# Spreading loads and stores of a Haar and convolution kernel over its pieces, and padding the rows of two inputs

## The chip, the cores and the metric

The kernel runs on one core of a Trainium2 chip. The metric is the device time of one execution in microseconds; lower is better. Engines are named as in the profile: PE is the matrix engine, PEld its weight loads, DVE the vector engine, ACT the scalar engine, POOL the general engine, and SP the engine that issues every DMA of this kernel.

## The reference

An image batch `x` of shape (4, 64, 256, 256) passes through four layers. Layers 0, 2 and 3 are global convolutions of each channel with a separable filter, computed by a small network of sines and a decay; the reference does it with transforms of twice the length, and adds `x` times a bias. Layer 1 works in the Haar domain:

```python
f1 = haar2d(x)
acc = jnp.zeros_like(f1[:, :conv_w.shape[1]])
for i in range(v.shape[0]):
    f3 = f1 * v[i]
    f4 = jnp.einsum('bchw,oc->bohw', f3, conv_w[i])
    f5 = jnp.sign(f4) * jax.nn.relu(jnp.abs(f4) - tau[i])
    acc = acc + f5
y = haar2d(acc, inverse=True)
return y + x
```

`v` and `tau` have one value for each of the 256 x 256 coefficients; `conv_w` mixes the 64 channels, for each of two terms `i`.

## The kernel before, in words

Everything is 32-bit floating point. The convolutions are products with triangular Toeplitz matrices, first along rows and then along columns; a tile of a filter's Toeplitz matrix (`toep`) is loaded from a table of repeated filters in DRAM. The batch is cut into two groups of two images each (`GROUPS`, `NB`), a group into 32 rounds of two channels (`ROUNDS`, `CI`). One round's tile has 128 partitions of 8 x 256 values, 8 KB to a partition, 1 MB in all.

There are three phases, written as lists of pieces of Python code that issue instructions:

- Phase a, 64 rounds: load `x`, convolve (matmuls `a1ps` and `a2ps`, ACT copies, DVE adds the bias term), Haar along rows on POOL (L341, L343), Haar along columns on PE (`a3ps`, L305), scale on DVE (L474), store to `coef` in DRAM.
- Phase b, once for each group, 64 steps of 128 units: load coefficients of all channels (`ft`, L545) and a step's `v` and `tau` (L557, one tile `v`), mix the channels on PE (L603, result in one PSUM tile `f4`), multiply by `v` on DVE (L622), sign and magnitude on ACT (L628, L637), subtract `tau` and threshold on DVE (L642, L647), add on POOL (L662, L665, L666), store to `mixed` (L671). For the second group half of the units skip the threshold: they are copied (L619) and stored to `unshrunk` (L679), and are thresholded late, in phase c.
- Phase c, 64 rounds of 18 pieces j = 0 to 17: load `g` from `mixed` in four DMAs of 256 KB (L746), scale it on ACT (L359), inverse Haar along rows on POOL (L382, result `ci`), along columns on PE (`c0ps`), then the last two convolutions (`c1r`, `c1c`, `c2r`, `c2c`), and store `out` (L867).

The function `beside` interleaves two lists: after each piece of the main list it issues as many pieces of the side list as keep both in proportion. Phase b of the first group runs beside phase a of the second group; phase b of the second group runs beside phase c of the first group; phase c of the second group runs alone. Every engine executes its instructions in the order in which the pieces issue them, so the place of a call in a piece is the place in the engine's queue. SP has one queue as well: a DMA that waits for a buffer or for its data holds up all DMAs issued after it. `AHEAD` is 3, and `alone` is 32, the first round of the second group.

Pools give a tile one of `bufs` buffers in turn; `ft` has four, `v` three, `g` three, `out` two. `load_f(s + 3)` loads the coefficients for three steps later and has to wait until POOL has added the previous step's, which read the same buffer. In phase c, piece (t, j) handles several rounds at once: it loads `g` for round t + 3 and scales it, runs POOL's steps for round t + 2, and the second convolution and the store for round t − 2.

Of the kernel before, what the change touches and what calls it, by code (L numbers as in the profile page):

```python
# [41 lines left out]
F32 = mybir.dt.float32  # L42
# [5 lines left out]
P = 128  # L48
B, C, N = 4, 64, 256

ROW = 64
BLOCKS = N // ROW
# [13 lines left out]
GROUPS = 2  # L66
NB = B // GROUPS
CI = 4 // NB
M = CI * NB

ROUNDS = C // CI
HALVES = 2 * ROUNDS
STEPS = C
# [4 lines left out]
AHEAD = 3  # L78
SHRINK = (1, 2, 3, 5, 6, 10, 11, 12, 14, 15)
W = 2 * N  # L80
# [4 lines left out]
IMAGES = (GROUPS, NB, ROUNDS, CI, BLOCKS, ROW, N)  # L85
TO_ROUNDS = (0, 2, 1, 5, 3, 4, 6)
# [4 lines left out]
C2 = float(np.float32(round((2.0 * math.pi - C1) * 2**21) / 2**21))  # L91
# [5 lines left out]
def conv_haar_kernel(  # L97
    ctx: ExitStack, tc: tile.TileContext, x, zT, w1, wbd, cols, wo, decay, wo_first, decay_first, bias, forward, inverse, wrow, pack, v, v_rows, out
):
    nc = tc.nc  # L100
# [7 lines left out]
    def coefficients(name):  # L108
        return dram.tile([CI, STEPS // 2, PAIR], F32, tag=name, name=name)

    coef = [coefficients(f"coef{g}") for g in range(GROUPS)]
    mixed = [coefficients(f"mixed{g}") for g in range(GROUPS)]
# [9 lines left out]
    def big(tag, name, bufs):  # L122
        return ac.tile([P, 2 * M, N], F32, tag=tag, name=name, bufs=bufs)

# [13 lines left out]
    def load_x(t):  # L138
        grp, r = divmod(t, ROUNDS)
        xs = big("in", f"x_{t}", 3)  # L140

        n = CI if grp == 0 else 2 * M
        for k in range(0, 2 * M, n):
            nc.sync.dma_start(xs[:, k : k + n], x[grp, r, :, k : k + n])
        return xs

    def load_toeplitz(l, t):
# [172 lines left out]
    def forward_free(src, dst, name):  # L320
# [4 lines left out]
        while half > 0:  # L325
            sums = nxt = None
            if half > 1:
                nxt = ac.tile([P, 2 * M, half], F32, tag=f"h{half}", name=f"{name}{half}", bufs=1)
                sums = nxt
# [25 lines left out]
    def scales(src):  # L355

        half = 2
        while half < N:
            nc.scalar.mul(diffs(src, half), diffs(src, half), math.sqrt(half))  # L359
            yield  # L360
            half *= 2

    def inverse_free(src, dst, name, engine):
# [5 lines left out]
        while half < N:  # L369
            o = dst  # L370
            if half < HALF:
                o = ac.tile([P, 2 * M, 2 * half], F32, tag=f"h{2 * half}", name=f"{name}{2 * half}", bufs=1)
            d = diffs(src, half)
# [27 lines left out]
    def run(ops, count):  # L401
        for _ in range(count):
            next(ops, None)

    def all_rows(grp_tile, r, images, joined):

        parts = images.rearrange("(m q) (h n) k -> q m h (n k)", q=2, h=2)
        n = NB * W
        pairs = []
        for q in range(2):  # L410
            for h in (slice(0, 2),) if joined else (slice(0, 1), slice(1, 2)):
                at = grp_tile.offset + ((h.start * 2 + q) * ROUNDS + r) * n
                rows = [[PAIR, P // 2], [2 * ROUNDS * n, h.stop - h.start], [1, n]]
                pairs.append((bass.AP(grp_tile.tensor, at, rows), parts[q][:, h]))
        return pairs
# [105 lines left out]
    def phase_b(grp):  # L521
# [4 lines left out]
        def raw(u):  # L526
            return grp == GROUPS - 1 and u % 2 == 1 and FULL <= u // 2 < STEPS
        st = [dict() for _ in range(STEPS)]
# [10 lines left out]
        def load_f(s):  # L539
            if s >= STEPS:  # L540
                return
            d = st[s]
            d["f"] = bp.tile([P, NB, W], F32, tag="ft", name=f"ft_{grp}_{s}", bufs=4)
            rows, f = step_of(coef[grp], s, d["f"])
            nc.sync.dma_start(f, rows)  # L545

        def load_v(s):
            if s >= STEPS:
                return
            d = st[s]  # L550
            d["v"], d["tau"] = [], []

            def fetch(first, count, tag):
                n = 2 * count * W
                t = bp.tile([P, count, 2, W], F32, tag=tag, name=f"{tag}_{grp}_{first}_{s}", bufs=3)
                at = v.offset + s * P * 4 * W + first * 2 * W
                nc.sync.dma_start(t.rearrange("p i k w -> p (i k w)"), bass.AP(v.tensor, at, [[4 * W, P], [1, n]]))  # L557
                d["v"] += [t[:, i, 0] for i in range(count)]
                d["tau"] += [t[:, i, 1] for i in range(count)]

            fetch(0, 2 if grp < GROUPS - 1 else 1, "v")
            if grp == GROUPS - 1 and not raw(2 * s + 1):
                fetch(1, 1, "raw")
# [117 lines left out]
        def piece(u, j):  # L681

            s, i = divmod(u, 2)
            if j == 0:
                if u < units:
                    multiply(u)
                if 0 < u <= units:
                    less(u - 1)
                if 1 < u <= units + 1:
                    add(u - 2)  # L690
                if i == 0 and s == 3:
                    part()
                    store(0)
                    store(1)
                if i == 0 and s > 3 and not raw(2 * s - 3):
                    store(s - 2)
                if i and raw(2 * s - 1):
                    store(s - 1)
            elif j == 1:
                if u + 1 < units:  # L700
                    mix(u + 1)
                if u < units:
                    sign(u)
                if i and s < STEPS and grp == GROUPS - 1:
                    store_raw(s)
                if 0 < u <= units:
                    threshold(u - 1)
                if i == 0 and s > 0:

                    load_v(s + 2)  # L710
                    load_f(s + 3)
            else:
                if u < units:
                    magnitude(u)
                if i == 0 and s < STEPS:
                    exchange(s)
# [16 lines left out]
    def phase_c():  # L733


        total = GROUPS * ROUNDS
        alone = total - ROUNDS
        st = [dict() for _ in range(total)]

        def load(t):  # L740
            if t >= total:
                return
            st[t]["g"] = big("in", f"g_{t}", 3)
            st[t]["scales"] = scales(st[t]["g"])
            for rows, g in all_rows(mixed[t // ROUNDS], t % ROUNDS, st[t]["g"], False):
                nc.sync.dma_start(g, rows)  # L746

        def load_raw(t):
            if alone <= t < total:
                r = st[t]["raw"] = late["sb"].tile([P, 2 * M, N], F32, tag="raw", name=f"raw_{t}", bufs=2)  # L750
                for rows, to in all_rows(unshrunk, t % ROUNDS, r, False):
# [40 lines left out]
        def scaled(t, count):  # L792
            if count and 1 < t < total:
                run(st[t]["scales"], count)
# [68 lines left out]
        def store(t):  # L863
            if t < total - 1:
                n = 2 * CI if t < alone else CI
                for k in range(0, 2 * M, n):
                    nc.sync.dma_start(out[t // ROUNDS, t % ROUNDS][:, k : k + n], st[t]["y"][:, k : k + n])  # L867
            st[t].clear()

        R1, C2, R2, C1 = 0, BLOCKS + 1, 2 * BLOCKS + 1, 3 * BLOCKS + 2  # L870

        def piece(t, j):
            flush()
            if j == 0:
                if t == 0:
                    load(2)
                sums(t + 2)
            if j == (BLOCKS if t == 0 else 1):
                load(t + 3)
            if j == 2:  # L880
                filters(t + 1, 1)
            if j == C2 + BLOCKS + 1 and t > 1:
                store(t - 2)
            if j == R2 + BLOCKS:
                filters(t, 2)
            first = t == alone - AHEAD
            if t >= alone - AHEAD:
                if j == 0 and first:
                    load_raw(alone)
                    load_rows()  # L890
                if j == 2 and first:
                    scale_rows()
                if j == BLOCKS + 1:
                    load_raw(t + AHEAD + 1)
                shrink(t + AHEAD, j - 2 * first)
            if R1 <= j < R1 + BLOCKS:
                if t < total:
                    rows(t, 1, j - R1)
            elif C2 <= j < C2 + BLOCKS:
                if 1 < t:  # L900
                    columns(t - 2, 2, j - C2)
            elif R2 <= j < R2 + BLOCKS:
                if 0 < t <= total:
                    rows(t - 1, 2, j - R2)
            elif j >= C1:
                if t < total:
                    columns(t, 1, j - C1)
            else:
                product(t + 1, int(j > BLOCKS))
            if t == 0:  # L910
                scaled(3, 2 * (2 * BLOCKS <= j < C1))
                scaled(2, int(j > 0))
            else:
                scaled(t + 3, {8: 3, 9: 2, 15: 1, 16: 1}.get(j, 0))
            if j > 0:
                step(t + 2, 1)

# [40 lines left out]
    a, head = a[-2 * A_PIECES :], A_PIECES + BLOCKS  # L958
# [134 lines left out]
```

## Time and profile before

| what | value |
|---|---|
| median of 3 runs | 2593.26 us (2591.77 to 2598.52) |
| profiled execution | 2595.18 us, its span 2591.5 us |
| mean granted PE clock | 0.977 |
| PE busy | 2324.7 us, 90% |
| PE weight loads | 1892.3 us, 73% |
| DVE busy | 1858.3 us, 72% |
| ACT busy | 1329.6 us, 51% |
| POOL busy | 2067.0 us, 80% |
| DMA | 685.23 MB, mean 264 GB/s |

The busy share is a mean over stages with different limits. The profile also cuts the span into 40 slices of 64.8 us and gives each engine's busy share in tenths for each; these rows and the busy times of single stretches are what to read first. A wait list says which engine waited for which, with the time in total, the number of times and the longest. "issue" stands for time in which an engine waited for nothing that the profile shows.

### The profile page before, as it was taken

To read this page: it belongs to the slowest core of one execution; us is meant where nothing else is said; L and a number is where in the kernel's file an instruction comes from. 1 tells how busy PE (TensorE), PEld (TensorE's weight loads), DVE (VectorE), ACT (ScalarE), POOL (GpSimd) and SP (SyncE) were. 2 spreads that over 40 slices of the span, in tenths; PEclk is the share of its full clock that TensorE was granted. 3 is DMA by queue.
4 is the path that set the end of the run, shared out by engine and by line. 5 is a ranking of instruction groups with operands and counts; after the bars stand their busy time and mean duration, and the time that the engine had idled before them with its cause. 6 is when DMAs were issued, how large, how long until landed. Compare 5 with 4: busy or idle time off the path is not lost.

```text
span 2591.5 us, 118522 instructions
## 1 busy us (share of the span) xinstructions
PE 2324.7 (90%) x53292; PEld 1892.3 (73%) x53292; DVE 1858.3 (72%) x2049; ACT 1329.6 (51%) x2187; POOL 2067.0 (80%) x2428
## 2 busy tenths in 40 slices
PE   5999998778888888757999999999989999999999
PEld 4887787444454445546777787787889999999998
DVE  2555445799999999646677677667757787777863
ACT  1221112566666666225666666666656556555552
POOL 1898887899999999757676877767779999999991
PEclk8999999999999999978999999999999999999999
DMA  7676898699999999555998989889876666666653
GB/s 209 219 245 232 287 304 293 248 346 317 348 324 329 346 321 331 184 191 184 328 320 304 330 302 313 309 313 315 289 221 219 212 203 222 210 205 210 215 166 112
DMA packets 203676, 685.23 MB, mean 264 GB/s; under 512 B 29289, under 2 KB 30826, under 8 KB 190755
## 3 DMA queue, kind: packets, MB, share of 16 engines
q1 hardware_dynamic: 203171, 677.67, 76.6%
q8 instruction: 418, 6.85, 1.1%
q14 instruction: 87, 0.71, 0.1%
HBM read 427.93 MB, written 249.63 MB: 261 GB/s over the span
## 4 chain that ended last, share of the span: by engine, by line
PE 53%; DVE 17%; POOL 9%; DMA 9%; issue 6%; ACT 3%; SPq 1%; DVEq 0%; ACTq 0%; POOLq 0%
PE c2c L293 9%; PE c2r L293 9%; PE c1r L293 8%; PE c1c L293 7%; PE a1ps L293 6%; PE a2ps L293 5%; PE f L603 4%; PE c0ps L305 3%; DVE m L647 3%; DVE x L622 3%; DMA v<-in_v 3%; POOL fw L341 2%; DVE a L642 2%; POOL f L343 2%; PE a3ps L305 2%
## 5 line engine op out<-in xcount | busy, mean ns | idle before, releaser
L382 POOL TENSOR_TENSOR i<-i,g 128x16 f32<-128x16 f32 x744 | 411.9, 574 | 27.7 <-ACT g L359 0.6
L293 PEld LDWEIGHTS a2ps<-toep,ay 64*64 64x64 f32 x8192 | 309.6, 137 | 158.0 <-DVE f L474 85.5
L293 PE MATMUL a2ps<-toep,ay 64*64 64x128 f32 (+3 forms) x8192 | 357.5, 306 | 46.6 <-DVE f L474 41.8
L603 PE MATMUL f<-ft,mix 64*64 64x512 f32 x2048 | 297.6, 619 | 109.5 <-DVE x L622 96.7
L293 PEld LDWEIGHTS a1ps<-toep,x 64*64 64x64 f32 x8192 | 293.6, 134 | 88.1 <-issue 43.7
L293 PE MATMUL a1ps<-toep,x 64*64 64x128 f32 (+3 forms) x8192 | 339.0, 300 | 18.6 <-DMA x<-in_x 13.8
L293 PEld LDWEIGHTS c2c<-toep,ch 64*64 64x64 f32 x8192 | 309.7, 134 | 54.1 <-issue 19.1
L293 PEld LDWEIGHTS c1c<-toep,ch 64*64 64x64 f32 x8192 | 306.6, 134 | 52.8 <-issue 17.5
L382 POOL TENSOR_TENSOR ci<-i,g 128x1024 f32<-128x1024 f32 x124 | 336.3, 2732 | 4.6
L293 PE MATMUL c1r<-toep,z 64*64 64x256 f32 (+3 forms) x8192 | 320.4, 300 | 19.2 <-ACT z L827 10.8
L293 PEld LDWEIGHTS c1r<-toep,z 64*64 64x64 f32 x8192 | 299.4, 135 | 47.6 <-issue 22.4
L293 PE MATMUL c2c<-toep,ch 64*64 64x128 f32 (+3 forms) x8192 | 320.7, 299 | 9.6 <-ACT ch L839 6.5
L293 PE MATMUL c1c<-toep,ch 64*64 64x192 f32 (+3 forms) x8192 | 316.9, 298 | 9.3 <-ACT ch L839 7.0
L441 ACT COPY ay<-a1ps 128x512 f32<-128x512 f32 x256 | 137.4, 589 | 351.8 <-PE a1ps L293 351.2
L293 PE MATMUL c2r<-toep,cy 64*64 64x128 f32 (+3 forms) x8192 | 311.9, 297 | 6.5 <-issue 5.9
L293 PEld LDWEIGHTS c2r<-toep,cy 64*64 64x64 f32 x8192 | 294.2, 134 | 30.5 <-issue 18.8
L665 POOL TENSOR_TENSOR gt<-m,ft 128x512 f32<-128x512 f32 x128 | 163.3, 1276 | 185.5 <-DVE m L647 179.1
L628 ACT ACTIVATE m<-x 128x1024 f32<-128x1024 f32 x194 | 206.1, 1063 | 193.6 <-DVE x L622 86.2
L839 ACT COPY ch<-c2r 128x512 f32<-128x512 f32 x256 | 137.5, 590 | 239.2 <-PE c2r L293 238.9
L474 DVE TENSOR_TENSOR f<-a3ps,wrow_sb 128x512 f32<-128x512 f32 x256 | 161.3, 682 | 132.6 <-PE a3ps L305 132.6
L622 DVE TENSOR_TENSOR x<-f,v 128x1024 f32<-128x1024 f32 x192 | 233.4, 1216 | 21.2 <-PE f L603 20.4
L839 ACT COPY ch<-c1r 128x512 f32<-128x512 f32 x256 | 137.8, 593 | 205.4 <-PE c1r L293 205.0
(83 smaller groups left out, 4001.2 us busy)
## 6 DMA issues: line engine op xcount, KB each, us to landing
toep<-filt SPq DMA_DIRECT2D x384, 224.0 KB, 5.4
ft<-coef SPq DMA_DIRECT2D x128, 512.0 KB, 7.7
v<-in_v SPq DMA_DIRECT2D x64, 1024.0 KB, 9.1
mixed<-gt SPq DMA_DIRECT2D x128, 512.0 KB, 7.4
g<-mixed SPq DMA_DIRECT2D x256, 256.0 KB, 5.3
x<-in_x SPq DMA_DIRECT2D x128, 256.0 KB, 4.9
coef<-f SPq DMA_DIRECT2D x128, 256.0 KB, 4.3
x<-in_x SPq DMA_DIRECT2D x32, 1024.0 KB, 8.6
```

What stands on the lines that cost most here:

```text
L293: nc.tensor.matmul(ps[r][half(c), j % 2, k * ROW :], data[half(r), c, k, bass.ts(j, ROW)], t(r, c)[:, : N - k * ROW], start=k == 0, stop=k ...
L305: nc.tensor.matmul(ps[r][half(c)].rearrange("p h k -> p (h k)"), matrix[half(r)], pairs(r, c).rearrange("p h k -> p (h k)"), start=True, s ...
L341: nc.gpsimd.tensor_tensor(diffs, even, odd, ALU.subtract)
L382: engine.tensor_tensor(to, s, d, op)
L441: later(lambda y=y, ps=ps: nc.scalar.copy(y, ps))
L474: later(lambda f=f, ps=ps, w=w: nc.vector.tensor_tensor(f, ps, w, ALU.mult))
L603: nc.tensor.matmul(un[u]["f4"][half(q), b, :], mixers[0][half(r), bass.ts(i, C)], st[s]["f"][half(r), b], start=True, stop=True, tile_posi ...
L622: nc.vector.tensor_tensor(un[u]["x"], un[u]["f4"], both(u, "v"), ALU.mult)
L628: nc.scalar.activation(un[u]["m"], un[u]["x"], AF.Sign)
L647: nc.vector.scalar_tensor_tensor(un[u]["m"], un[u]["a"], 0.0, un[u]["m"], ALU.max, ALU.mult)
L665: nc.gpsimd.tensor_tensor(g[:, 0], m[:, 0], st[s]["f"][:, 0], ALU.add)
L839: later(lambda y=y, ps=ps: nc.scalar.copy(y, ps))
```

## The change

There are three parts.

First, the arrays `x` and `v` in DRAM get rows of 8 KB and 512 bytes of zeros, so that row starts are 8704 bytes apart and no longer 8192. The same bytes are loaded in DMAs of the same sizes. `out` keeps its shape.

Second, in phase c of the first group, the four loads of `g` for a round are issued in pieces 1, 3, 5 and 7 in place of all in piece 1 (except in round 0 and in the rounds from `alone - AHEAD` on); the two halves of a store of `out` are issued in pieces 10 and 12 in place of both in piece 10; and the first five scalings of `g` on ACT go from pieces 8 and 9 to pieces 11 and 12 in all rounds but round 0.

Third, in phase b of the second group, `load_f(s + 3)` moves from the second third of a step's first unit, directly behind `load_v(s + 2)`, to the last third of its second unit, four pieces later. In the first group it stays.

```diff
+PAD = 128
...
-            nc.sync.dma_start(xs[:, k : k + n], x[grp, r, :, k : k + n])
+            at = x[grp, r, :, k * N : (k + n) * N]
+            nc.sync.dma_start(xs[:, k : k + n].rearrange("p n k -> p (n k)"), at)
...
-                at = v.offset + s * P * 4 * W + first * 2 * W
-                nc.sync.dma_start(t.rearrange("p i k w -> p (i k w)"), bass.AP(v.tensor, at, [[4 * W, P], [1, n]]))
+                at = v.offset + s * P * (4 * W + PAD) + first * 2 * W
+                rows = bass.AP(v.tensor, at, [[4 * W + PAD, P], [1, n]])
+                nc.sync.dma_start(t.rearrange("p i k w -> p (i k w)"), rows)
...
                 if i == 0 and s > 0:
 
                     load_v(s + 2)
+                    if grp < GROUPS - 1:
+                        load_f(s + 3)
+            else:
+                if i and s > 0 and grp == GROUPS - 1:
                     load_f(s + 3)
-            else:
                 if u < units:
                     magnitude(u)
...
-        def load(t):
+        def load(t, k=slice(0, 4)):
             if t >= total:
                 return
-            st[t]["g"] = big("in", f"g_{t}", 3)
-            st[t]["scales"] = scales(st[t]["g"])
-            for rows, g in all_rows(mixed[t // ROUNDS], t % ROUNDS, st[t]["g"], False):
+            if k.start == 0:
+                st[t]["g"] = big("in", f"g_{t}", 3)
+                st[t]["scales"] = scales(st[t]["g"])
+            for rows, g in all_rows(mixed[t // ROUNDS], t % ROUNDS, st[t]["g"], False)[k]:
                 nc.sync.dma_start(g, rows)
...
-                    nc.sync.dma_start(out[t // ROUNDS, t % ROUNDS][:, k : k + n], st[t]["y"][:, k : k + n])
+                    stores.append(lambda k=k, y=st[t]["y"]: nc.sync.dma_start(out[t // ROUNDS, t % ROUNDS][:, k : k + n], y[:, k : k + n]))
             st[t].clear()
+            for put in stores[: len(stores) if t >= alone else 1]:
+                put()
+            del stores[: len(stores) if t >= alone else 1]
...
-            if j == (BLOCKS if t == 0 else 1):
-                load(t + 3)
+            if t == 0 or t >= alone - AHEAD:
+                if j == (BLOCKS if t == 0 else 1):
+                    load(t + 3)
+            elif j in (1, 3, 5, 7):
+                load(t + 3, slice(j // 2, j // 2 + 1))
+            if stores and j == C2 + BLOCKS + 3:
+                stores.pop(0)()
...
-                scaled(t + 3, {8: 3, 9: 2, 15: 1, 16: 1}.get(j, 0))
+                scaled(t + 3, {11: 3, 12: 2, 15: 1, 16: 1}.get(j, 0))
...
+    def padded(rows):
+
+        return f(np.concatenate([rows, np.zeros((*rows.shape[:-1], PAD), np.float32)], axis=-1))
...
-        "x": f(a["x"].reshape(IMAGES).transpose(TO_ROUNDS).reshape(GROUPS, ROUNDS, P, CI * BLOCKS, N)),
+        "x": padded(a["x"].reshape(IMAGES).transpose(TO_ROUNDS).reshape(GROUPS, ROUNDS, P, 2 * M * N)),
...
-        "v": f(np.repeat(v[:, :, None], C, axis=2)),
+        "v": padded(np.repeat(v[:, :, None], C, axis=2).reshape(STEPS * P, 4 * W)),
```

More of the change, by code (lines that the diff above doesn't have):

```diff
@@ L737, in phase_c @@
         alone = total - ROUNDS
+        stores = []
         st = [dict() for _ in range(total)]
-        def load(t):
+        def load(t, k=slice(0, 4)):
             if t >= total:
                 return
-            st[t]["g"] = big("in", f"g_{t}", 3)
-            st[t]["scales"] = scales(st[t]["g"])
-            for rows, g in all_rows(mixed[t // ROUNDS], t % ROUNDS, st[t]["g"], False):
+            if k.start == 0:
+                st[t]["g"] = big("in", f"g_{t}", 3)
+                st[t]["scales"] = scales(st[t]["g"])
+            for rows, g in all_rows(mixed[t // ROUNDS], t % ROUNDS, st[t]["g"], False)[k]:
                 nc.sync.dma_start(g, rows)
@@ L1086 @@
     ]
-    args.append(nc.dram_tensor("out", arrays["x"].shape, F32, kind="ExternalOutput").ap())
+    args.append(nc.dram_tensor("out", (GROUPS, ROUNDS, P, CI * BLOCKS, N), F32, kind="ExternalOutput").ap())
     with tile.TileContext(nc) as tc:
```

## The prediction

> **What bounds the kernel now.** I read the page's slices first, then the busy time by stretch, then the waits inside the stretches that are not full.
>
> ```profile
> PE   5999998778888888757999999999989999999999
> DVE  2555445799999999646677677667757787777863
> DMA  7676898699999999555998989889876666666653
> ```
>
> A slice is 64.8 us. There are four stages: the first group's forward rounds (slices 1 to 6), the second group's beside the first group's mixing (7 to 16), the first group's inverse beside the second group's mixing (18 to 29), and the second group's inverse alone (to the end). The change is aimed at the third.
>
> ```profile
> core 0: us, PE busy (x) PEld busy (x) DVE busy (x) ACT busy (x) POOL busy (x), PEclk, DMA share, GB/s
> 270.00:390.00 120.00, 112.62 (x2868) 96.41 (x2864) 58.05 (x88) 21.57 (x40) 100.86 (x175) 1.00 0.94 303
> 520.00:1000.00 480.00, 391.61 (x6380) 233.31 (x6372) 459.08 (x470) 311.40 (x386) 434.58 (x474) 0.99 0.95 334
> 1225.00:1850.00 625.00, 586.18 (x13752) 487.63 (x13756) 444.21 (x422) 396.38 (x691) 457.33 (x513) 0.99 0.91 317
> 1950.00:2560.00 610.00, 608.29 (x16508) 577.24 (x16504) 460.61 (x487) 339.64 (x631) 538.58 (x540) 1.00 0.63 200
> ```
>
> The last stage has PE busy 608.3 of 610 us: nothing there can be won. In the second, DVE is busy 459.1 of 480 us (96%); its largest wait in that stretch is 16.6 us for ACT's magnitude, in 30 waits of at most 0.9 us, and none of its listed waits is for a DMA. So DMA, though 95% busy, does not set that stage. The third stage belongs to PE, which idles 625.0 − 586.2 = 38.8 us:
>
> ```profile
> PE f L603 <- DVE x L622: 15.4, 14, 2.3
> PE c1r L293 <- issue: 7.6, 9, 1.6
> PE c2r L293 <- issue: 5.9, 6, 1.7
> PE c2c L293 <- issue: 3.0, 4, 1.4
> PE c1c L293 <- issue: 2.2, 4, 0.9
> PE f L603 <- issue: 2.0, 1, 2.0
> ```
>
> (columns: us, times, longest). "issue" sums to 20.7 us in 24 stalls; 15.4 us are DVE being late with `x`. The second kind is no matter of transfers: before several of these, L642 (mean 1582 ns here, 1233 ns in the second stage) had taken over 2 us while POOL ran its 128x1024 step of L382 (mean 2816 ns).
>
> What is "issue"? PE's instructions come through DMA queue 8 (page: 418 packets, 6.85 MB, so 16 KB each). In the packet records PE's longer issue stalls mostly begin and end around such a packet and end 1.3 to 1.45 us after it lands. One case: packets of queue 8 start at 1506.5, 1510.8 and then only 1518.3, a gap of 7.5 us where 625/108 = 5.8 us is the mean; PE stalls 1.28 us from 1519.25. What SP had issued just before:
>
> ```profile
> 1506.47 3.28 SPq L746 DMA_DIRECT2D g<-mixed  x4
> 1509.85 1.20 SPq L155 DMA_DIRECT2D toep<-filt  x2
> 1511.15 1.01 SPq L557 DMA_DIRECT2D v<-in_v  x1
> 1512.27 0.54 SPq L545 DMA_DIRECT2D ft<-coef  x1
> 1513.27 0.57 SPq L671 DMA_DIRECT2D mixed<-gt  x1
> 1514.32 1.05 SPq L679 DMA_DIRECT2D unshrunk<-raw  x1
> ```
>
> That is 1024 + 448 + 4 x 512 = 3520 KB in 8.9 us, 405 GB/s asked of engines that move 317 in this stage. Other stalls (1532.4, 1456.3, 1634.1) also follow a burst of `g`; I take the backlog of a burst to hold up the fetch.
>
> **What the Trainium skill says.** *Runtime: NRT & Kernel Launch*, "Instruction fetch mechanics": the sequencer streams instructions in 16 KiB blocks through its own DMA queue, mostly hidden. The trace agrees on size and queue, not on hidden. *DMA: Bandwidth & Descriptors*, "Queues, rings and completion order": an engine alternates between its queues by packet, so a backlog should delay a fetch little; the 7.5 us gap above speaks against that, without proving what delayed it. The same page, "Latency and other measured facts": row pitches at large powers of two slowed copies, a few KiB of padding cured it and +192 B did not; its pitches start at 512 KiB. Here the pitch is 8 KB and the pad 512 B, so it is only a hint. The packet records add to it: in 520 to 1000 us an 8 KB packet (`v`, `x`) takes 309 ns at the median but 391 in the mean, 581 at the ninetieth percentile, while 4 KB packets (159, 170, 169) in the same stretch hardly vary. Yet rows of `ft` and `mixed` lie 4 KB apart, a power of two as well, so that the pitch is the cause is open. *SBUF — State Buffer*, "Who interferes with whom": a DVE instruction with two SBUF inputs blocks against a GpSimd one that reads SBUF; the 1582 ns of L642 agree.
>
> **The change part by part.** The sum is against the profiled execution, 2595.2 us (span 2591.5); the median of the three runs, 2593.3, lies 1.9 below it.
>
> *Padded `x` and `v`.* The same packets, 512 B apart. If the 8 KB mean falls from 391 to some 320 ns, the second stage's DMA share falls by 9125 x 71 ns / 16 / 480 us = 8 points, and buys nothing, because DVE's order of work repeats there every 9.4 us: 0 us (+3 to −5). In the first stage 2 KB packets take 106 ns where the median is 84: 0.26 of the share becomes 0.21, and 0.94 falls to some 0.89. PE idles 7.4 us in 270 to 390, 5.8 of it issue, 1.6 for `x`; I take −3 (0 to −7). At the start PE waits 9.3 us for `x`, behind the broadcast of the filters: −1 (0 to −3). In the third stage `v` is 58 x 128 packets of 4 KB; a saving of 40 ns each is 7424 x 40 ns / 16 = 19 us of 625, 3 points of 91, counted with the next part.
>
> *Loads of `g` in pieces j = 1, 3, 5, 7; half of `out` two pieces later; `ft` four pieces later.* Every issue remains (0.5 to 0.6 us of SP each, SP is not full); what goes is three of four `g` loads out of a burst, one of two stores, and `ft` from behind `v`. A round takes some 25.5 us here (24 rounds from the `g` load at 1222.7 to that at 1835.1), a piece 1.4 us, so 1024 KB are asked for over 8.5 us in place of 3. SP now waits 56.3 us at `ft` (L545) for POOL's L665, and toep, `g` and `out` queue behind it. After the move it meets the same event two pieces later at the store of `mixed` (L671, now 19.0 us on POOL), when it has mostly happened: that wait shrinks, and the store of `out` (L867, 99.5 us for DVE `o`), which only follows its producer, stays. `ft` is used two steps on, some 18 us after its new place, and lands in 7.2. I take half of the 20.7 us of issue stalls away: −10 (0 to −20). What is late next is DVE: its 15.4 us stay, and could grow a little where PE comes sooner.
>
> *Scales at j = 11, 12 instead of 8, 9.* The same ACT instructions. The last `g` load has four pieces, 5.7 us, to land before the first scale; before, the last of the burst had 6.6 to 13 us as read from the trace, and ACT waited for it only once after 1300 us (1.7 us). It lands in 6.2 now, alone a little sooner, and SP is usually ahead by some us. Behind ACT's wait stand the sign, magnitude and copies, then DVE's L642. +1 (0 to +12). POOL takes up the tile only in the next round, after all scales.
>
> *Transitions and last stage.* Loads of the last rounds keep their burst; the 7.1 us that ACT waits at 1885 stay: 0 (±2).
>
> Sum: −1 − 3 + 0 − 10 + 1 = −13, so 2582.2 for the profiled execution and **2580 us** as a median.
>
> **The rivals.** *Nothing moves* (24%): the fetch is late for a reason of its own, or DMA stays at 0.9 because no byte is taken away. For it: the second stage has 0.95 without harm to DVE; queues alternate by packet. Against: the last stage, at 0.63, has no issue stall listed although PE uses up instructions faster there. It gives −2 to 0 beside the first stage: about 2592. *ACT waits for the fourth `g`* (14%): it decides when landing exceeds 5.7 us plus SP's lead. With a landing of 9.4 (the longest in this stage before) and no lead, 3.7 us in each of some 25 rounds are 92 us of ACT, which idles 37%; if DVE and PE take over a fifth of it, +18, less 5 won: 2606, slower. The 1.7 us once speak against. *All of it goes* (10%): issue stalls vanish in both stages and some of `x`: −3 − 7 − 20 − 3 = −33, 2560. The forecast itself has 52%, 2571 to 2588. That the padding does nothing is a part of the first rival.
>
> **How the numbers follow.** I take 0.3%, 7.8 us, as what a measurement of this kernel can tell from no change; faster is below 2585.5. Of the forecast's 52% some 44 lie below; with the 10 and a little of the first rival, 56%. Slower: 14 and 2 of the rest, 16%. Same: 28%. The range leaves out the upper part of the slow rival and the tail below all stalls gone: 2560 to 2601.
>
> **What would show it.** Right: 8 KB packets near 320 ns in the mean; DMA share below 0.89 and "issue" near 10 us in 1225 to 1850; L545's wait for POOL gone; the second stage's step still 9.4 us. Wrong: "issue" at 20 us with `g` spread (first rival); ACT `g` <- DMA `g` above 25 us (second); the second stage shorter by over 5 us, which would mean that DMA did set it.

## The result and the profile after

The changed kernel takes 2586.21 us (median of 13 runs) beside 2594.36 us for the kernel before (13 runs on the same chip): a ratio of 0.9964 with a 95% interval of 0.995 to 0.9977. That is 0.36% or some 9 us (the medians lie 8.2 us apart); the forecast was 13. The profiled execution has a span of 2583.6 us against 2591.5 before, 7.9 less. The total came out nearly right, and by luck: the time was won in another place than the one forecast.

The slices of the kernel after, in the rows shown of before:

```profile
PE   5999999678888888757999999999989999999999
DVE  2555445799999999646677777766757777777763
DMA  7676998699999999555988999988876666666653
```

In slices 18 to 29, at which the spreading was aimed, PE's row is as it was. DMA's row there is no lower. The same stretches as before, by busy time:

```profile
core 0: us, PE busy (x) PEld busy (x) DVE busy (x) ACT busy (x) POOL busy (x), PEclk, DMA share, GB/s
270.00:390.00 120.00, 113.52 (x2870) 95.27 (x2866) 57.10 (x87) 21.81 (x41) 100.36 (x175) 1.00 0.95 311
520.00:1000.00 480.00, 390.73 (x6382) 231.96 (x6372) 459.07 (x470) 311.36 (x386) 434.60 (x474) 0.99 0.95 334
1225.00:1850.00 625.00, 586.26 (x13670) 480.16 (x13666) 442.48 (x420) 393.28 (x686) 449.56 (x510) 0.99 0.91 315
1950.00:2560.00 610.00, 610.00 (x16828) 557.63 (x16823) 430.93 (x494) 340.97 (x640) 544.04 (x542) 1.00 0.63 203
```

First, the third stage (third row): PE is busy 586.26 us where it was 586.18, DMA's share is 0.91 as before, and the matmuls in the stretch are 13670 where they were 13752. Nothing was won there. Second, the last row: PE's busy time rises by 1.7 us only, but the count in brackets goes from 16508 to 16828 matmuls in the same 610 us, 1.9% more work, and DVE's busy time falls by 30 us. The last stage became faster, and a busy share of 99.7% had hidden that there was something to win.

Cutting the trace at matmuls that stand for the same work in both kernels (the first mixing matmul, the first `c0ps`, the `c0ps` with which round 32 begins, the last matmul) gives each stage's length:

| stage | before, us | after, us | difference |
|---|---|---|---|
| first group's forward rounds | 436.8 | 435.4 | −1.4 |
| second group's forward rounds beside mixing | 681.0 | 682.5 | +1.5 |
| first group's inverse beside mixing | 817.4 | 820.3 | +2.9 |
| second group's inverse alone | 651.7 | 640.8 | −10.9 |

The differences sum to −7.9, the difference of the spans. Against my sum: −4 was forecast for the first stage, −9 for the third, 0 for the last.

PE's waits in 1225 to 1850 us after the change:

```profile
PE f L607 <- DVE x L626: 12.2, 12, 2.7
PE c1r L296 <- issue: 11.7, 14, 2.4
PE c1c L296 <- issue: 3.5, 5, 1.1
PE f L607 <- issue: 2.7, 3, 1.6
...
PE c2c L296 <- issue: 1.5, 3, 0.9
PE c2r L296 <- issue: 1.1, 2, 0.8
```

"issue" sums to 20.5 us in 27 stalls; before it was 20.7 us in 24. Spreading the bursts took none of it away. ACT's waits in the same stretch answer the rival that ended slower:

```profile
...
ACT g L362 <- DMA g<-mixed: 0.3, 1, 0.3
```

ACT waits 0.3 us for a load of `g`, once (10.4 us in three waits before). So ACT loses nothing by the later landing.

**Where the last stage won.** Half a round takes 9.59 us there, as the distance between `c0ps` pairs. Before, 14 of the 64 took 10.2 or 10.5 us; those are seven rounds with about 1.55 us lost in each, 10.9 us. After, none did. One of them, at 2105 us, in the timeline of before:

```profile
start us, us, engine line op out<-in xcount [idle before <-releaser]
...
2104.28 1.61 ACT L359 ACTIVATE g<-g 128x512 f32<-128x512 f32 x2
...
2105.96 4.69 POOL L806 TENSOR_TENSOR g<-g,shrunk 128x1024 f32<-128x1024 f32 x2 [0.43 <-ACT g L359]
...
2108.33 3.42 DVE L781 TENSOR_TENSOR x<-raw,rows 128x1024 f32<-128x1024 f32 x1
...
2111.84 1.03 ACT L783 ACTIVATE shrunk<-x 128x1024 f32<-128x1024 f32 x1 [1.55 <-DVE x L781]
...
2113.70 0.59 ACT L839 COPY ch<-c1r 128x512 f32<-128x512 f32 x1
```

The columns are start, duration, engine, line and operation, with the wait ahead of it in brackets. POOL's row is two instructions of 128x1024 in 4.69 us; in the instruction records the second begins at 2108.29 and lasts 2.36 us. DVE's L781, which also reads two SBUF operands, starts at 2108.33, 0.04 us behind it, and takes 3.42 us in place of 1.22, its shortest in this stage: the 2.32 us that POOL's instruction still has to run, and 1.10 us more. ACT stands 1.55 us idle for its result, and ACT's copy `ch`, queued behind, is late for PE's weight loads. The same round in the timeline of after:

```profile
start us, us, engine line op out<-in xcount [idle before <-releaser]
...
2104.66 1.62 ACT L362 ACTIVATE g<-g 128x512 f32<-128x512 f32 x2
...
2106.36 5.68 POOL L815 TENSOR_TENSOR g<-g,shrunk 128x1024 f32<-128x1024 f32 x2 [0.47 <-ACT g L362]
...
2108.20 1.62 DVE L790 TENSOR_TENSOR x<-raw,rows 128x1024 f32<-128x1024 f32 x1
...
2110.05 1.04 ACT L792 ACTIVATE shrunk<-x 128x1024 f32<-128x1024 f32 x1
...
2111.90 1.10 ACT L848 COPY ch<-c1r 128x512 f32<-128x512 f32 x2
```

PE's `c1r` begins at 2106.57 before and at 2106.50 after, so the two timelines can be laid over each other. ACT's last scaling of `g`, which releases POOL, ends 0.39 us later, and POOL starts 0.40 us later: the five moved scalings, 0.55 and 0.61 us of ACT's time, now stand among the copies just ahead of it (at 2101.37 and 2102.74), while before they ran in a gap at 2094.28. DVE arrives while POOL's first instruction is still running, goes next, and takes 1.62 us; now POOL's pair is the one that is stretched, to 5.68 us, and no half round is longer for it. ACT's copy `ch` comes 1.8 us earlier. The Trainium skill says in *SBUF — State Buffer*, "Who interferes with whom", that a DVE instruction with two SBUF inputs contends with a GpSimd (POOL) one that reads SBUF, and that the order of issue decides which of the two is blocked. The two timelines agree.

So do the records of all fourteen traces of this case, 64 of these DVE instructions in each. 580 of the 896 took over 1.3 us; every one of them started while a POOL instruction ran, and took the rest of that instruction plus 1.08 to 1.10 us. Only at the very start of a POOL instruction can DVE still go first: of the 45 that started less than 0.025 us behind it, 44 took under 1.3 us; of the 45 from 0.025 to 0.045 us, 20 did; of the 166 from there to 0.3 us, none. The kernel before stands on this edge: up to 0.032 us behind, its L781 took 1.23 us, and from 0.035 us on some 3.4. In the kernel after, L781 starts some 0.5 us ahead of POOL's second addition. All rounds of this stage on that line, first before, then after:

```profile
L781 DVE TENSOR_TENSOR x<-raw,rows x58: 1223/1780/3424, 1951.8 to 2509.5; 128x1024 f32<-128x1024 f32 x58
...
  ACT shrunk L783: 28.5, 29
```

```profile
L790 DVE TENSOR_TENSOR x<-raw,rows x59: 1283/1616/1773, 1945.2 to 2501.5; 128x1024 f32<-128x1024 f32 x59
```

The three numbers are the shortest, median and longest duration in ns. Over 3 us were 15 of 64 before and 1 of 64 after (in the whole stage, whose first microseconds the lines leave out). Eight of the 15 waited for a POOL instruction of L806 and seven, each directly after one of these, for the `ci` step of L382, also 128x1024: a slow round is such a pair. ACT waited for the line 29 times, 28.5 us, and after the change not at all. What reached PE is less than that, because PE loses nothing by waits of ACT that end in time; and it shows as waits of weight loads of 0.3 to 0.4 us, in 1950 to 2560 us of before:

```profile
PEld c1c L293 <- ACT ch L839: 4.7, 14, 0.4
PEld c2c L293 <- ACT ch L839: 2.0, 7, 0.3
```

The same list of after has neither line.

### The profile page after: what moved, and what is told of

Same layout as the page of the kernel before. It is cut to its first block, busy times and chain, and to the rows that moved or that the text cites. A ratio compares the mean times of both kernels' runs of the same rounds, so it can differ in the third digit from the quotient of the medians.

```text
span 2583.6 us, 118458 instructions
## 1 busy us (share of the span) xinstructions
PE 2319.3 (90%) x53292; PEld 1848.1 (72%) x53292; DVE 1823.0 (71%) x2049; ACT 1324.7 (51%) x2187; POOL 2064.4 (80%) x2428
## 4 chain that ended last, share of the span: by engine, by line
PE 60%; DVE 14%; POOL 10%; DMA 6%; issue 5%; ACT 3%; SPq 2%; DVEq 0%; ACTq 0%; POOLq 0%
PE c2c L296 11%; PE c2r L296 10%; PE c1r L296 9%; PE c1c L296 9%; PE a1ps L296 6%; PE a2ps L296 6%; PE f L607 4%; PE c0ps L308 4%; POOL fw L344 3%; DVE m L651 3%; POOL f L346 3%; DVE x L626 3%; DVE a L646 2%; PE a3ps L308 2%; DVE x L464 2%
## 5 line engine op out<-in xcount | busy, mean ns | idle before, releaser
L385 POOL TENSOR_TENSOR i<-i,g 128x16 f32<-128x16 f32 x744 | 431.5, 601 | 27.7 <-ACT g L362 0.6
L296 PE MATMUL a1ps<-toep,x 64*64 64x64 f32 (+3 forms) x8192 | 337.6, 300 | 16.6 <-DMA x<-in_x 11.4
L296 PEld LDWEIGHTS c2c<-toep,ch 64*64 64x64 f32 x8192 | 300.0, 135 | 58.9 <-issue 19.1
L296 PE MATMUL c1r<-toep,z 64*64 64x192 f32 (+3 forms) x8192 | 319.0, 300 | 22.6 <-issue 11.9
L296 PEld LDWEIGHTS c1c<-toep,ch 64*64 64x64 f32 x8192 | 296.2, 134 | 57.8 <-issue 18.5
L296 PE MATMUL c2c<-toep,ch 64*64 64x256 f32 (+3 forms) x8192 | 314.7, 299 | 8.4 <-ACT ch L848 6.8
L296 PE MATMUL c1c<-toep,ch 64*64 64x128 f32 (+3 forms) x8192 | 310.3, 298 | 9.0 <-ACT ch L848 5.5
L385 POOL TENSOR_TENSOR ci<-i,g 128x1024 f32<-128x1024 f32 x124 | 313.9, 2552 | 4.5
L296 PE MATMUL c2r<-toep,cy 64*64 64x192 f32 (+3 forms) x8192 | 310.1, 297 | 1.3 <-issue 1.1
L626 DVE TENSOR_TENSOR x<-f,v 128x1024 f32<-128x1024 f32 x192 | 233.5, 1216 | 22.1 <-PE f L607 20.5
L344 POOL TENSOR_TENSOR fw<-x 128x1024 f32<-128x1024 f32 x64 | 122.2, 1910 | 150.4 <-DVE x L464 137.9
```

The source lines that it names most:

```text
L296: nc.tensor.matmul(ps[r][half(c), j % 2, k * ROW :], data[half(r), c, k, bass.ts(j, ROW)], t(r, c)[:, : N - k * ROW], start=k == 0, stop=k ...
L344: nc.gpsimd.tensor_tensor(diffs, even, odd, ALU.subtract)
L385: engine.tensor_tensor(to, s, d, op)
L626: nc.vector.tensor_tensor(un[u]["x"], un[u]["f4"], both(u, "v"), ALU.mult)
```

## The experiments

The theory after the result: the gain comes from the place of the scalings alone, through the order of arrival of DVE's L781 and POOL's 128x1024 instructions in the last stage (*the port*). Its rivals: the padding gives it (*the padding*), or the spread transfers do, by a smaller backlog (*the backlog*). "Late scalings" are those at j = 11, 12 from round `alone - AHEAD` = 29 on only, so in the last stage but not in the third; `only_late_scales` and `pad_late` with its variants have them (`pad_late_g` in the third stage too). Ratios are to the kernel before on the same chip; "slow halves" counts half rounds of the last stage over 9.9 us, "L781 over 3 us" instructions of 64, and "issue" PE's stalls of that name in 1225 to 1850 us, each in the one profiled execution.

| kernel | ratio (95%) | third stage, us | issue, us | last stage, us | slow halves | L781 over 3 us |
|---|---|---|---|---|---|---|
| before | 1 | 817.4 | 20.7 | 651.7 | 14 | 15 |
| after | 0.9964 (0.995 to 0.9977) | 820.3 | 20.5 | 640.8 | 0 | 1 |
| only_late_scales | 0.9944 (0.9924 to 0.9964) | 815.5 | 18.2 | 641.0 | 0 | 1 |
| all_but_late_scales | 0.9998 (0.9983 to 1.0013) | 825.5 | 24.7 | 652.0 | 15 | 15 |
| padding_only | 0.9954 (0.9938 to 0.9969) | 808.3 | 11.8 | 653.4 | 16 | 17 |
| no_v | one run, 2574.29 us | 793.8 | 2.6 | 652.2 | 14 | 17 |
| pad_late | 0.9941 (0.9918 to 0.9964) | 825.5 | 20.2 | 642.5 | 2 | 1 |
| pad_late_g | 0.9964 (0.9948 to 0.998) | 814.3 | 16.4 | 640.8 | 0 | 1 |
| pad_late_ft | 0.9939 (0.9915 to 0.9963) | 809.5 | 16.3 | 641.3 | 1 | 1 |
| pad_late_out | 0.9944 (0.9924 to 0.9965) | 812.0 | 16.6 | 640.8 | 0 | 1 |
| split_sums | 0.9963 (0.9949 to 0.9977) | 818.8 | 23.2 | 640.9 | 0 | 0 |
| pad_x | 0.9996 (0.9985 to 1.0007) | 816.8 | 19.3 | 648.9 | 10 | 12 |
| pad_v | 0.9996 (0.9982 to 1.0009) | 811.1 | 13.4 | 640.8 | 0 | 1 |
| pad_scales | 0.9945 (0.9927 to 0.9962) | 811.6 | 11.9 | 640.8 | 0 | 1 |

**only_late_scales**: the kernel before, with nothing changed but this:

```diff
-                scaled(t + 3, {8: 3, 9: 2, 15: 1, 16: 1}.get(j, 0))
+                early = t < alone - AHEAD
+                scaled(t + 3, ({8: 3, 9: 2, 15: 1, 16: 1} if early else {11: 3, 12: 2, 15: 1, 16: 1}).get(j, 0))
```

> The kernel before, with one edit: from round 29 on the first five scalings of g run in pieces 11 and 12 instead of 8 and 9. Theory A (the gain comes from the last stage alone: the scalings shift ACT's last scaling and so POOL's additions by some 0.4 us, so that DVE's L781 no longer loses the shared read port to a 2.2 us POOL instruction, and ACT's copies of ch are no longer late for PE): the whole gain, 0.9964 of before within 0.002, the last stage about 641 us instead of 652, no wait of PE's weight loads for ACT's ch after 1950 us. Theory B (spreading the transfers and padding the rows gave it): 1.000 within 0.0015, last stage 652 us.

It measured 0.9944. The line's durations in the last stage are those of after:

```profile
L781 DVE TENSOR_TENSOR x<-raw,rows x59: 1247/1609/1760, 1943.6 to 2500.1; 128x1024 f32<-128x1024 f32 x59
```

The scalings' place in the last stage by itself gives the 10.7 us there, and a total at least as good as the whole change.

**all_but_late_scales**: the reverse, the kernel after with the scalings of the last stage put back.

```diff
-                scaled(t + 3, {11: 3, 12: 2, 15: 1, 16: 1}.get(j, 0))
+                early = t < alone - AHEAD
+                scaled(t + 3, ({11: 3, 12: 2, 15: 1, 16: 1} if early else {8: 3, 9: 2, 15: 1, 16: 1}).get(j, 0))
```

> The changed kernel, with the scalings of g back in pieces 8 and 9 from round 29 on; padding and the spread of g, out and ft stay. Theory A: the gain is gone, 1.000 within 0.002, and the rounds with 10.2 and 10.5 us in place of 9.6 are back in the last stage. Theory B: the gain stays, 0.9964, because the transfers are as in the changed kernel.

It measured 0.9998, no gain at all, and the slow rounds are back:

```profile
L790 DVE TENSOR_TENSOR x<-raw,rows x59: 1223/2002/3427, 1951.2 to 2518.7; 128x1024 f32<-128x1024 f32 x59
...
  ACT shrunk L792: 28.5, 29
```

So all that was forecast to give 13 us, the padding, the spread loads and stores and the moved `ft`, gives together nothing that can be measured.

**split_sums**: the kernel before with the scalings at 8 and 9, and POOL's two instructions of L806 cut into four of half the size. This tests the port itself, without touching the scalings.

```diff
-                    for h in range(2):
-                        to, of = (s[k].rearrange("p (s n) k -> p s (n k)", s=2)[:, h] for k in ("g", "shrunk"))
+                    for h in range(4):
+                        to, of = (s[k].rearrange("p (s n) k -> p s (n k)", s=4)[:, h] for k in ("g", "shrunk"))
```

> The kernel before, with POOL's additions of shrunk to g in the second group cut from two instructions of 128x1024 (2.35 us each) into four of 128x512; the scalings stay in pieces 8 and 9. Theory A (DVE's L781 loses the shared port to one long POOL instruction): L781 can wait for at most some 1.3 us of them, the slow half rounds go from 14 to at most 3, the last stage takes 641 to 644 us, ratio about 0.996. Theory B (the late scalings free ACT itself, which then copies ch in time): last stage 652 us, 14 slow half rounds, ratio 1.000.

It measured 0.9963. DVE's line in the last stage:

```profile
L781 DVE TENSOR_TENSOR x<-raw,rows x58: 1226/1296/2314, 1952.6 to 2499.5; 128x1024 f32<-128x1024 f32 x58
...
  ACT shrunk L783: 6.8, 15
```

None is over 3 us now. 16 of 64 are over 2.2 us; 15 of these start 0.05 to 0.07 us behind a POOL instruction of L382 of half the size (128x512, 1.28 us) and wait for its end, and they cost PE nothing: no half round is slow. The last stage takes 640.9 us with the scalings where they were. A second edit, which shortens what DVE waits for and leaves the scalings alone, has the same effect as the first. With the law of the durations above I count the port as shown.

**padding_only**: the kernel before with padded `x` and `v`, the first part of the change and nothing else.

> The kernel before with nothing but the padded rows of x and v. Theory A: 1.000 within 0.0015, and the 8 KB packets keep a mean of about 390 ns between 520 and 1000 us. Theory B with the padding as its cause: 0.997 or less and 8 KB packets near 320 ns.

It measured 0.9954, more than I had expected, although its last stage has all the slow rounds. Its 8 KB packets take 388 ns in the mean where before has 391, so the padding does not do what it was to do. In its one trace 9.1 us of the gain lie in the third stage and 3.6 in the first. The 2 KB packets of `x` in 270 to 390 us go from 106 to 99 ns. To see which array it is, each was padded alone.

**pad_x** and **pad_v** (`padding_only` with one of its two arrays put back):

> The kernel before with padded rows of x alone. Theory A (padding acts on the 2 KB pieces of x in the first stage and nowhere else): the first stage about 4 us shorter, 0.9985, as much as padding of both apart from chance. Theory B (v's rows matter in the third stage): 1.000 to 0.9985 here and the larger part with pad_v.

> The kernel before with padded rows of v alone. Theory A: 1.000 within 0.0015, first stage as before. Theory B: 0.997, third stage shorter by 6 us or more with fewer issue stalls.

Both measured 0.9996, no change. The two do not add up to the 0.9954, and `pad_late` against `only_late_scales` (0.9941 and 0.9944) shows no effect of the padding either. The first stage takes 433.1 to 436.9 us (mean 434.7) in the eight traces with both padded and 436.1 to 440.1 (mean 438.2) in the six with one or none, so some 3 us there may be real; the 2 KB packets take 98 to 101 ns in the nine with `x` padded and 103 to 106 in the five without. What the rest of `padding_only`'s gain was stays open. `pad_v` carries a warning besides: its scalings are at 8 and 9, yet its profiled execution (2581.05 us, the second fastest of its 14 runs) has no slow half round, while its runs as a whole are no faster. There L781 starts 0.012 to 0.030 us behind POOL's second addition in every second half round from 1950 us on and goes first each time: the same edge as in `before`, on its lucky side. Which engine goes first need not be the same in every execution, and one profile does not tell how often the race is lost.

**no_v**: the kernel before, in which the second group's mixing uses the `v` and `tau` loaded for step 2 in all later steps, so that these loads (1 MB or less for each step) and the result they would give are left out.

```diff
+            if grp == GROUPS - 1 and s >= 3:
+                d["v"], d["tau"] = kept
+                return
```

> The kernel before, but phase b of the second group loads v and tau only for its first three steps and uses those of step 2 for all later ones, so its output is not the reference's. It takes 58 of the 512 KB loads, 15 percent of the bytes, out of the third stage. If PE's issue stalls there come from the backlog of transfers: DMA share about 0.78 in 1225 to 1850 us and issue on PE falls from 20.7 to below 8 us. If they have another cause: 15 us or more stays.

The stretch 1225 to 1850 us, and the waits of PE in it:

```profile
1225.00:1850.00 625.00, 598.50 (x14212) 477.83 (x14216) 460.01 (x436) 409.58 (x712) 487.26 (x529) 0.99 0.79 276
```

```profile
PE f L609 <- DVE x L628: 17.9, 18, 2.5
...
PE c1r L293 <- issue: 1.8, 4, 0.6
...
PE c1c L293 <- issue: 0.8, 1, 0.8
```

With DMA's share at 0.79 instead of 0.91, "issue" falls from 20.7 us to 2.6, the matmuls in the stretch rise from 13752 to 14212, and the third stage takes 793.8 us. DVE's lateness stays (17.9 us, 15.4 before). In the other traces, at a share of 0.89 to 0.91, "issue" lies between 11.8 and 24.7 us, so this one run stands well outside them. PE's issue stalls do come with the load on the DMA engines: taking loads away, their bytes and their number at once, took the stalls away, and spreading the same loads did not. By what path the load acts is open, for a packet of queue 8 takes as long here as before (1.06 and 1.08 us in the mean).

**pad_late** (the padding and the late scalings) is the base for the three parts of the spreading:

> The kernel before with padding, and with the late scalings (pieces 11 and 12) from round 29 on; no transfer is spread. Theory A (two gains that add up: padding alone measured 0.9954, late scalings alone 0.9944): 0.990, some 2570 us, third stage 808 us, last stage 641 us. Theory B (the two shorten the same thing): 0.994 to 0.995.

It measured 0.9941, theory B's number: the two gains do not add up. Its profiled execution was a long one (span 2588.8 us, third stage 825.5), so it is its ratio that counts here; its two slow half rounds stand beside no L781 over 3 us, and their cause is open. **pad_late_g** adds to it the spread loads of `g`, and with them the scalings at 11 and 12 in the third stage too; **pad_late_ft** the moved `load_f`; **pad_late_out** the halves of `out` apart, each as in the change.

> As pad_late, and the four loads of g in pieces 1, 3, 5, 7 with the scalings in 11 and 12 from round 1 on. Theory A (spreading makes issue stalls worse, and the g loads are most of the spread bytes): about 0.994, third stage 815 to 820 us, issue on PE back to 20 us from about 12. Theory B (one of the other moves does it): 0.990, third stage 808 us.

> As pad_late, and ft's load of the second group moved behind the store of unshrunk, four pieces later. Theory A (the spread of g does the harm): 0.990, third stage within 3 us of pad_late. Theory B (ft's move does it, since its wait for POOL had paced SP, or since it now stands behind the waits for mixed and unshrunk): 0.994, third stage longer by 8 us or more.

> As pad_late, and the second half of each store of out two pieces later. Both theories: 0.990 within 0.0015, third stage within 3 us of pad_late, since a store that is never waited for in time moves by 2.8 us. A loss of over 6 us would say that the store in piece 12 does harm where it lands.

The 0.990 in these three texts was theory A's number for `pad_late`, and none of them reached it. The move of `ft` (0.9939) and the halves of `out` (0.9944) make no difference to 0.9941. The spread `g` has 0.9964, the same as the whole change and above the number of either theory; its third stage (814.3 us) and its "issue" (16.4 us) do not show why. **pad_scales**, the padding with the scalings at 11 and 12 in every round and no spreading, separates the loads of `g` from their scalings:

> Padding, and the scalings of g in pieces 11 and 12 from round 1 on, with g, out and ft issued as in the kernel before. Theory A (the loads of g apart from one another cost something in the third stage, the scalings do not): as pad_late, 0.994. Theory B (the later scalings do the harm there): as pad_late_g, 0.9964.

It measured 0.9945. So the scalings in the third stage cost nothing that shows, and if something costs some 0.2% it is the loads of `g` in pieces. `after` (0.9964) against the versions without them (0.9939 to 0.9945), and `all_but_late_scales` (0.9998) against `padding_only` (0.9954), point the same way. The intervals of the first comparison overlap, and in the second `out`, `ft` and the scalings of the third stage differ too, so this is likely and not shown; by what path it would act I do not know, for `pad_late_g` has no longer a third stage than the others in its trace. The kernels with late scalings and without the spread `g` have the lowest ratios: 0.9939 to 0.9945, some 0.2% below the kernel after.

## Why the prediction was right, and where it was not

The measured median is 6 us above the 2580 that were forecast, inside the range. The kernel became faster, which was held the likeliest, but barely by the prediction's own measure: 2586.21 lies above the 2585.5 at which it let "faster" begin, while the medians on one chip lie 8.2 us apart, just over its 7.8. That the total fits is luck, as its own steps show:

- *Transitions and last stage: 0 (±2).* **This step failed.** It measured −10.9 us. I took PE's 608.3 us of 610 to mean that nothing could be won. The Trainium skill warns of this in *Perfetto Trace Analysis*, at its head and in "Identifying the Most-Contended Engine": matmul busy time is a bad measure of headroom, because matmuls are pipelined. I had not used it; the traces agree, 1.7 us of busy time for 320 matmuls. The number of matmuls in the stretch (16508 before, 16828 after) is what shows it; the busy time of the weight loads, which fell from 577.24 to 557.63 us, does not. The trace of before had the other signs: L781 with a longest of 3.42 us against 1.22, ACT 28.5 us waiting for it. I had used the rule of the two-operand instructions for L642 in the third stage and did not ask where else it holds.
- *Scales at j = 11, 12: +1 (0 to +12).* I priced them by what they wait for, the load of `g`; that part held (0.3 us). Who waits for them I dismissed with "POOL takes up the tile only in the next round, after all scales". But the last scaling, at j = 16, is what releases POOL's L806 (0.43 us of wait in the timeline above), it came 0.4 us later, and that shift is what took DVE off the edge. The step had the wrong sign and missed its place: −10.7 us by `only_late_scales`.
- *Spread `g`, `out` and `ft`: −10 (0 to −20).* Failed: "issue" 20.7 to 20.5 us, third stage +2.9. That the stalls come with the load on the DMA engines was right, as `no_v` shows (20.7 to 2.6 us); that bursts make them was not. The error was to take half of it away by moving the same bytes about. The trace of before spoke against bursts of `g` already: of its ten issue stalls of over 0.9 us in this stretch, five ended over 11 us after the last load of `g` was issued, the prediction's own case at 1519.25 among them. (What it read of the landing holds: all ten ended 1.3 to 1.6 us after a packet of queue 8 had landed.) I had this as the first rival's own argument, "DMA stays at 0.9 because no byte is taken away", and as an argument against the forecast it was right. L545's wait for POOL did go, as forecast, and SP waits elsewhere: 38.2 us for POOL at the store of `mixed` (19.0 before) and 27.8 us for PE's `c1c` at `toep` (0.6 before).
- *8 KB packets 391 to some 320 ns.* Failed: 389. The second stage's step stays 9.4 us, its DVE busy 459.1 us; that it does not depend on DMA was forecast but, with DMA's share still 0.95, it was not put to the test.
- *First stage −4 (start and 270 to 390 us).* −1.4 in this pair of traces, some −3 over all of them. The 2 KB packets did get a little shorter, 106 to 101 ns, far less than the 84 that I had taken: that was the median, and the median stayed at 84.
- *The slow rival* (ACT waits for the fourth `g`) fell by the 0.3 us.

The first rival, nothing moves, was right that nothing moves in the third stage; of its two reasons, `no_v` speaks against a fetch that is late for a reason of its own. Its total was beaten only by an effect that none of the cases held. Two misses cancelled, by luck: −10 in the third stage that did not come, and −11 in the last that nobody had looked for.

## What to carry to other kernels

Where a stretch is "full", compare the work done in it (matmuls for each microsecond, or the spacing of one marker instruction from round to round), since a busy engine may be slowed from outside. Look for one line whose longest duration is two or three times its shortest: where it is a two-operand instruction of DVE beside a long one of POOL, cutting the long one in two or shifting one of them by some half a microsecond is a cheap edit; either one took all slow half rounds away here. Read the distance between the two starts as well: a kernel that wins by 0.01 us is not safe. And when PE's "issue" grows with the load on DMA, take loads away; spreading the same bytes did nothing here.

## What the runs showed of the hardware that was not expected

- In the kernel before, L781 took 1.23 us where it started up to 0.032 us behind POOL's 128x1024 instruction and some 3.4 us from 0.035 us on; in seven rounds of 32 that carried through to 1.55 us of the round.
- Whoever comes second waits for the whole rest: L781 took what was left of POOL's instruction plus 1.08 to 1.10 us, in 580 cases of 580.
- Small waits on that line cost PE nothing (`split_sums`: 15 of them, 6.8 us, 0.45 us each in the mean, and no slow half round). The chain over DVE and ACT has that much slack here before PE feels it.
- PE loses 20.7 us of 625 to "issue" at a DMA share of 0.91 (11.8 to 24.7 in the thirteen traces at 0.89 to 0.91), and 2.6 us at 0.79, in one run.
- The third stage's length differs by 17 us between profiles of kernels that differ little (808.3 to 825.5 us), and longer ones have more "issue" as a rule (11.8 us and 24.7 us at these two). A difference of a few microseconds there, in one trace each, is no finding.
